# A two-layer graph attention kernel: edges counted block by block, two weight sums made by DMA, the range check moved back

## The chip, the core and the metric

The kernel runs on one core of a Trainium2 chip. Its engines are TensorE (PE; its weight loads are listed as PEld), VectorE (DVE), ScalarE (ACT), GpSimd (POOL) and SyncE (SP), each with an instruction queue of its own that is worked off in order. DMA transfers are issued from the queues of SP, ACT and POOL. The metric is the device time of one execution in microseconds. Three runs of the kernel before the change took 659.91, 660.31 and 660.65 us, so the median is 660.31 us.

## What is computed

The reference is a two-layer graph attention network (8 heads, then 1 head) on 512 nodes with 768 features, followed by a residual and a layer norm. There are 16,896 edges, sorted by destination; every node has a loop to itself.

```python
def gat_layer(x, W, a_s, a_d, b, edge_index, concat):
    h = (x @ W).reshape(n, H, C)
    src, dst = (edge_index[0], edge_index[1])
    alpha_s = jnp.einsum('nhc,hc->nh', h, a_s)
    alpha_d = jnp.einsum('nhc,hc->nh', h, a_d)
    e = jax.nn.leaky_relu(alpha_s[src] + alpha_d[dst], NEG_SLOPE)
    m = jax.ops.segment_max(e, dst, num_segments=n)
    e = jnp.exp(e - m[dst])
    denom = jax.ops.segment_sum(e, dst, num_segments=n)
    alpha = e / (denom[dst] + EPS)
    msg = h[src] * alpha[:, :, None]
    return jax.ops.segment_sum(msg, dst, num_segments=n) + b

h = jax.nn.elu(gat_layer(x, W1, a_src1, a_dst1, b1, edge_index, concat=True))   # 8 heads of 768
out = gat_layer(h, W2, a_src2, a_dst2, b2, edge_index, concat=True)             # 1 head of 768
x = _layernorm(x + out)
```

## The kernel before

**Edges become a matrix.** Instead of gathering by edge, the kernel counts how many edges lead from each source to each destination. The result `cnt` is 512 x 512; attention is then dense arithmetic on it. The edges are cut into 132 chunks of 128. DVE writes, for each chunk, a one-hot tile of the sources, `os` (128 edges x 512 nodes, L418), and for a quarter of the chunks at once a one-hot tile of the destinations, `odw` (L409). TensorE multiplies the two and adds the products up in PSUM (L430), 32 destination rows at a time, on one of four groups of 32 columns of the array (`tile_position=(0, r)`), so that products on different groups can run beside each other.

**Two blocks for every chunk.** As the edges are sorted, a chunk lies near a known destination. Nodes come in 16 blocks of 32. `first[c]` is the first of two neighbouring blocks that chunk `c` is counted into. `odw` is 64 columns wide for each chunk (`W = 2 * B`), and each chunk costs two products: 264 in all. `rel` (L201) is the destination less the first node of those blocks.

**The range check.** L203 and L205 count the edges whose `rel` is outside 0 to 63 into `stray`. A product with a column of ones (L444) sums this over the partitions, L459 copies the sum to `flag`, and L482 loads it into a register of every engine. Where it is not zero, the whole pass is done again by a general path (`flag is None`); otherwise that path is skipped.

**Order of the first stage.** The order in each queue is written out by hand. `order` lists the chunks in waves of up to four, `batches` takes four waves at a time, and the loop at L454 does for each batch: destinations if needed, the sources of its chunks, some DVE work from `extra` (sums of `x`, logits of head 0, and in the last batches `tsums`), then on TensorE the `items` that are due (the projection of head 0 and the first four pieces of that of head 1, each six matmul records; transposes of `x` by `turn_x` at the positions in `turns`), then `count`. `os` has 28 buffers: DVE can't write the 29th before TensorE has read the first. When all four rows of blocks of a `cnt` tile are done, ACT copies it out (`counted`, L337, L338). In the last batch `spread` (L363) and `lift` (L369) come ahead of the last count; then DVE does `leak` (L373) and `rank` (L378) for the softmax, and TensorE goes on with the projection of head 1.

**Strassen's products.** Projections use seven half-size products instead of eight (Winograd's form; P1 to P7). On the right-hand side they need sums of quarters of the weight matrix: T1 = B11 + B12, T3, T2 = T1 + B22, T4 = T2 + B21. `load_w` makes T1 and T3 with accumulating DMAs from POOL's queue (L104, L115); `right` returns T2 and T4 as two DVE additions (L240, L241). For head 1 these are the `tsums` that stand in batches 8 and 9 of the first stage. P6 reads T2 and P4 reads T4; both come after the first four pieces.

**The rest.** For heads 0 to 7 the kernel then aggregates (L625, L571), applies the ELU, multiplies by the head's part of the second weight matrix (L248) and projects the head after next (L248). None of this is touched, apart from its start.

**Before the first product.** TensorE runs 13 products on zeros (`keep_warm(13)`), turns the indices (L181), runs one more on zeros, transposes a tile of `x` (L327), runs two on zeros, does the range check's product (L444), runs two more on zeros, and starts the projection of head 0 (L352).

Of the kernel before, what the change touches and what calls it, by code (L numbers as in the profile page):

```python
# [36 lines left out]
def gat_pass(  # L37
# [134 lines left out]
    nc.vector.memset(far, -NO_EDGE)  # L172


    idx_f = ohp.tile([EH, 2, 2, P], F32, name="idx_f")
    nc.vector.tensor_copy(idx_f, idx_i)
    idx = ohp.tile([P, 2, EC], F32, name="idx")
    psi = tr.tile([P, 512], F32, name="tr")
    for j in range(2):
        for r in range(2):  # L180
            nc.tensor.transpose(psi[:, (2 * j + r) * EH:(2 * j + r + 1) * EH], idx_f[:, j, r, :],  # L181
                                ident[:EH, :EH])
    nc.vector.tensor_copy(idx, psi[:, :2 * EC].rearrange("p (j c) -> p j c", j=2))

    general = flag is None


    B = 32
    W = 2 * B
    first = [min(max(round(((c + 0.5) * P * N / E) / B - 1), 0), N // B - 2) for c in range(EC)]  # L190
    runs = []
    for c in range(EC):
        if not runs or first[c] != first[runs[-1][0]]:
            runs.append([c, c])
        runs[-1][1] = c + 1
    if not general:
        base = ohp.tile([P, EC], F32, name="base")
        for lo, hi in runs:
            nc.gpsimd.memset(base[:, lo:hi], float(first[lo] * B))
        rel = ohp.tile([P, EC], F16, name="rel")  # L200
        nc.vector.tensor_tensor(rel, idx[:, 0, :], base, op=ALU.subtract)  # L201
        below = ohp.tile([P, EC], F16, name="below")
        nc.vector.tensor_scalar(below, rel, 0.0, None, op0=ALU.is_lt)  # L203
        stray = const.tile([P, 1], F32, name="stray")
        nc.vector.scalar_tensor_tensor(below, rel, float(W), below, op0=ALU.is_ge, op1=ALU.add,  # L205
                                       accum_out=stray)

    cnt = keep.tile([P, NT, N], F32, name="cnt")
    absent = keep.tile([P, NT, N], BF16, name="absent")
# [24 lines left out]
    def right(W_, slot):  # L234
        lo, hi, t1 = W_
        b11, t3, b21, b22 = lo[:, :, L], lo[:, :, R], hi[:, :, L], hi[:, :, R]
        t2, t4 = (wpool.tile([P, HK, HALF], F32, name=f"{slot}t{j}") for j in (2, 4))
        tt = nc.vector.tensor_tensor
        return dict(P1=b11, P2=b21, P3=b22, P4=t4, P5=t1, P6=t2, P7=t3), [
            lambda: tt(t2, t1, b22, op=ALU.add),  # L240
            lambda: tt(t4, t2, b21, op=ALU.add),  # L241
        ]
# [76 lines left out]

    load_w1(1, "w2")()  # L320


    def turn_x(t):
        for ks in (range(4), range(4, DC)):
# [55 lines left out]
        nc.scalar.activation(q, q, AF.Exp, bias=nmax, scale=-1.0)  # L380
        return q

    order = []
    for g in range(NT):
        rs = [list(range(lo, hi)) for lo, hi in runs if lo * NT // EC == g]
        while any(rs):
            order.append([r.pop(0) for r in rs if r])
    def turn_b1():
        psb = mm.tile([P, 512], F32, name="mm")
        nc.tensor.transpose(psb[:, :H * DC], b1_rows, ident[:H * DC, :H * DC])  # L390
# [1 line left out]
        nc.scalar.activation(nb1T, psb[:, :H * DC], AF.Copy, scale=-1.0)  # L392

    XA, xsums = left(xT, xS)
    B1, tsums = right(W1[1], "w2")
    items = whole_projection(0)
    again = None
    if not general:
        hits = {}
        for c in range(EC):  # L400
            for k in range(2):
                hits[first[c] + k] = hits.get(first[c] + k, 0) + 1
        todo = dict(hits)
        cps, done = {}, 0
        od = ohp.tile([P, EC, W], BF16, name="odw", bufs=1)

        def destinations(lo, hi):
            hi = min(hi, EC)
            nc.vector.tensor_tensor(od[:, lo:hi, :],  # L409
                                    rel[:, lo:hi].unsqueeze(2).to_broadcast([P, hi - lo, W]),  # L410
                                    nodes[:, :W].unsqueeze(1).to_broadcast([P, hi - lo, W]),
                                    op=ALU.is_equal)

        def sources(wave):
            hot = {}
            for c in wave:
                hot[c] = ohp.tile([P, N], BF16, name="os", bufs=28)
                nc.vector.tensor_scalar(hot[c], nodes, idx[:, 1, c:c + 1], None, op0=ALU.is_equal)  # L418
            return hot

        def count(wave, hot):
            nonlocal done
            for k in range(2):
                for c in wave:
                    b = first[c] + k
                    t, r = b * B // P, b * B % P
                    if t not in cps:
                        pool, name = (bc, "bc") if t == 2 else (tr, "tr")
                        cps[t] = pool.tile([P, 512], F32, name=name)
                    nc.tensor.matmul(cps[t][r:r + B, :N], od[:, c, k * B:(k + 1) * B], hot[c],  # L430
                                     start=todo[b] == hits[b], stop=todo[b] == 1,
                                     tile_position=(0, r), skip_group_check=True)
                    todo[b] -= 1
            while done < NT and all(todo[b] == 0 for b in range(done * P // B, (done + 1) * P // B)):
                counted(done, cps[done])
                done += 1


        turns = {1: 3, 5: 0, 9: 1}
        keep_warm(1)  # L440
        turn_x(2)
        keep_warm(2)
        pst = tr.tile([P, 512], F32, name="tr")
        nc.tensor.matmul(pst[:1, :1], stray, ones, start=True, stop=True)  # L444
        keep_warm(2)
        wholes = len(items)

        extra = {2: xsums[:1], 4: [lambda: logits(0, HS[0], 2)],
                 5: [xsums[1], lambda: logits(0, HS[0], 3)], 6: [*xsums[2:], lambda: logits(0, HS[0], 0)],
                 7: [lambda: logits(0, HS[0], 1)], 8: tsums[:1], 9: tsums[1:]}  # L450
        BW = 4
        batches = [order[i:i + BW] for i in range(0, len(order), BW)]
        pos, ready, quarter = 0, 0, EC // NT
        for n, batch in enumerate(batches):  # L454
            while ready <= max(c for wave in batch for c in wave):
                destinations(ready, ready + quarter)
                ready += quarter
            if n == 0:
                nc.vector.tensor_copy(flag, pst[:1, :1])  # L459
            hot = [sources(wave) for wave in batch]  # L460
            for f in extra.pop(n, []):
                f()
            want = min(2 + ((n + 1) * (wholes + 4) * BW + len(order) - 1) // len(order), wholes + 4)
            while pos < want:
                if pos == wholes:
                    pairs = projection(1, XA, B1)
                    items += [lambda p=p: (p[0](), p[1]()) for p in pairs[:4]]
                if pos in turns:
                    turn_x(turns[pos])
                items[pos]()  # L470
                pos += 1
            if n == 2:
                turn_b1()
            if n + 1 == len(batches):
                spread(0)
                q = [lift(0, t) for t in range(NT)]
                for t in range(NT - 1):
                    leak(q[t])
                for t in range(NT - 1):
                    rank(q[t], t)  # L480
            if n == 1:
                again = nc.values_load(flag[:1, :1], min_val=0, max_val=E)  # L482
            for wave, h_ in zip(batch, hot):
                count(wave, h_)
        assert not extra and pos == len(items) and done == NT
    else:
        for t in range(NT):
            ps = mm.tile([P, 512], F32, name="mm")
            for c in range(EC):
                o1 = ohp.tile([P, P], BF16, name="od", bufs=4)  # L490
                o2 = ohp.tile([P, N], BF16, name="os", bufs=28)
                nc.vector.tensor_scalar(o1, nodes[:, t * P:(t + 1) * P], idx[:, 0, c:c + 1], None,
                                        op0=ALU.is_equal)
                nc.vector.tensor_scalar(o2, nodes, idx[:, 1, c:c + 1], None, op0=ALU.is_equal)
                nc.tensor.matmul(ps[:, :N], o1, o2, start=c == 0, stop=c == EC - 1)
            counted(t, ps)
            turn_x(t)
        turn_b1()
        for f in items + xsums + tsums:
            f()  # L500
        for t in range(NT):
            logits(0, HS[0], t)
        pairs = projection(1, XA, B1)
        for m, e in pairs[:4]:
            m()
            e()
        spread(0)
        q = [lift(0, t) for t in range(NT)]
        for t in range(NT - 1):
            leak(q[t])  # L510
        for t in range(NT - 1):
            rank(q[t], t)
# [426 lines left out]
```

## Time and profile before

| what | us | where from |
|---|---|---|
| median of 3 runs | 660.31 | times |
| the profiled execution's own time | 660.2 | its record |
| span, first to last instruction | 658.4 | page |
| outside the span | 1.8 | 660.2 - 658.4 |
| first product of head 0's projection starts | 8.70 | chain in order of time |
| last product of the last count but one ends | 68.1 | chain in order of time |
| product of head 1's P6 (first after the counts) starts | 69.23 | timeline |

In the profile, a time in front of a line is microseconds from the start of the span. A group's own time includes its latency, so groups of back-to-back instructions are best measured from the start of one group to the start of the next. "[3.04 <-PE tr L430]" after a line means that its engine was idle for 3.04 us just before it and that a TensorE instruction of line 430 released it. One f32 product is listed as two records.

### The profile page before, as it was taken

What the parts mean: (1) busy time and instruction counts of PE and PEld (TensorE: products, weight loads), DVE (VectorE), ACT (ScalarE), POOL (GpSimd) and SP (SyncE); (2) the same over time, 40 slices, a digit from 0 to 9 for tenths busy, and PEclk for the clock granted to TensorE, in tenths of its full rate; (3) what the DMA queues carried; (4) which work ended last, traced back from release to release, by engine and by line L of the source; (5) the groups of instructions that cost most, each with busy time, mean ns of one, the idle gap of its engine ahead of it and who ended that gap; (6) DMA issues with size and microseconds to landing.
All of it is one profiled execution on the core that took longest, in us unless ns stands there. A gap on an engine that the chain in (4) does not pass through costs nothing.

```text
span 658.4 us, 7115 instructions
## 1 busy us (share of the span) xinstructions
PE 649.1 (99%) x2419; PEld 402.0 (61%) x2419; DVE 511.2 (78%) x1102; ACT 248.7 (38%) x417; POOL 42.4 (6%) x52
## 2 busy tenths in 40 slices
PE   9999999999999999999999999999999999999995
PEld 5555577556865577556855576556755545644553
DVE  6989989977779587767779687867776589866775
ACT  2222646350635135440726135430726043333440
POOL 1200011010100110010000110011000000000000
PEclk9999999999999999999999999999999999999998
DMA  8801299177803982087604790196506865000132
GB/s 311 237 1 49 33 276 278 41 223 156 224 1 68 247 235 66 16 243 187 169 0 110 205 265 35 32 255 201 129 0 166 211 201 133 24 0 1 32 57 77
DMA packets 71355, 85.58 MB, mean 130 GB/s; under 512 B 36566, under 2 KB 55950, under 8 KB 71310
## 3 DMA queue, kind: packets, MB, share of 16 engines
q1 hardware_dynamic: 59022, 66.76, 32.6%
q0 software_dynamic: 12000, 17.70, 15.9%
q10 hardware_dynamic: 288, 0.59, 0.3%
q8 instruction: 21, 0.34, 0.2%
q14 instruction: 24, 0.20, 0.1%
HBM read 75.07 MB, written 1.57 MB: 116 GB/s over the span
## 4 chain that ended last, share of the span: by engine, by line
PE 95%; DVE 3%; ACT 0%; DMA 0%; issue 0%; DVEq 0%; ACTq 0%
PE mm L248 59%; PE mm L625 17%; PE mm L571 6%; PE mm L352 5%; PE mm L891 3%; PE tr L430 2%; PE bc L154 1%; PE bc L430 1%; PE bc L363 1%; DMA zr<-nr 0%; DVE q L373 0%; DVE q L378 0%; DVE q L528 0%; PE mm L327 0%; PE tr L819 0%
## 5 line engine op out<-in xcount | busy, mean ns | idle before, releaser
L248 PE MATMUL mm<-w,gT 128*128 128x384 f32 x288 | 97.4, 487 | 0.0
L248 PE MATMUL mm<-w,xT 128*128 128x384 f32 x252 | 83.9, 487 | 0.0
L248 PEld LDWEIGHTS mm<-w,gT 128*128 128x128 f32 x288 | 53.9, 190 | 35.7 <-issue 2.0
L248 PEld LDWEIGHTS mm<-w,xT 128*128 128x128 f32 x252 | 47.7, 190 | 33.7 <-PE bc L430 0.4
L248 PE MATMUL mm<-w1t,gS 128*128 128x384 f32 x180 | 60.7, 486 | 0.0
L380 ACT ACTIVATE q<-q,nmax 128x512 f32<-128x512 f32 x36 | 25.8, 722 | 89.8 <-DVE nmax L378 89.8
L248 PE MATMUL mm<-w2t,xS 128*128 128x384 f32 x168 | 56.6, 487 | 0.0
L625 PE MATMUL mm<-PT,hs 128*128 128x256 f32 x216 | 52.6, 379 | 0.0
L629 ACT COPY u<-mm 128x256 f32<-128x256 f32 x18 | 6.7, 372 | 119.0 <-PE mm L625 119.0
L306 DVE TENSOR_TENSOR h<-h,mm 128x384 f32<-128x384 f32 x72 | 39.6, 551 | 14.4 <-PE mm L248 13.8
L248 PEld LDWEIGHTS mm<-w1t,gS 128*128 128x128 f32 x180 | 34.1, 190 | 23.6
L248 PEld LDWEIGHTS mm<-w2t,xS 128*128 128x128 f32 x168 | 31.8, 190 | 22.2 <-issue 0.2
L625 PEld LDWEIGHTS mm<-PT,hs 128*128 128x128 f32 x216 | 41.0, 190 | 7.2 <-issue 0.4
L548 ACT COPY nr<-q 128x1024 uint16<-128x1024 uint16 x32 | 33.4, 1044 | 22.5 <-DVE q L534 15.5
L571 PE MATMUL mm<-PT,hs 128*128 128x512 f32 x96 | 41.6, 593 | 0.0
L418 DVE TENSOR_SCALAR os<-nodes,idx 128x512 bf16<-128x512 f16 x132 | 36.0, 345 | 3.0 <-PE tr L430 3.0
L553 ACT COPY PT<-zr 128x1024 uint16<-128x1024 uint16 x32 | 37.1, 1158 | 2.0 <-DMA zr<-nr 2.0
L625 PE MATMUL mm<-pS,gS 128*128 128x256 f32 x144 | 37.1, 380 | 0.2 <-DVE pS L598 0.2
L352 PE MATMUL mm<-w,xT 128*128 128x384 f32 x96 | 33.2, 493 | 0.0
L248 PE MATMUL mm<-w,gS 128*128 128x384 f32 x96 | 32.6, 486 | 0.0
L248 PE MATMUL mm<-w1t,gT 128*128 128x384 f32 x96 | 32.5, 487 | 0.0
L571 PEld LDWEIGHTS mm<-PT,hs 128*128 128x128 f32 x96 | 18.2, 190 | 22.9 <-issue 21.5
(158 smaller groups left out, 1031.5 us busy)
## 6 DMA issues: line engine op xcount, KB each, us to landing
w<-in_L_gnn_W_dram SPq DMA_DIRECT2D x90, 384.0 KB, 6.2
w<-in_L_gnn_W_dram POOLq DMA_DIRECT2D x15, 576.0 KB, 8.7
w2t<-in_L_gnn_W_dram SPq DMA_DIRECT2D x8, 576.0 KB, 4.6
w2t<-in_L_gnn_W_dram POOLq DMA_DIRECT2D x8, 576.0 KB, 8.7
w1t<-in_L_gnn_W_dram SPq DMA_DIRECT2D x7, 576.0 KB, 4.4
w1t<-in_L_gnn_W_dram POOLq DMA_DIRECT2D x7, 576.0 KB, 9.4
a_s<-in_L_gnn_a_src_dram SPq DMA_DIRECT2D x8, 384.0 KB, 3.6
a_d<-in_L_gnn_a_dst_dram SPq DMA_DIRECT2D x8, 384.0 KB, 3.6
```

The lines of the kernel that those rows point to most:

```text
L248: nc.tensor.matmul(ps[:, :HALF], A_[p][:, k, i * P:(i + 1) * P], B_[p][:, k, :], start=start and k == 0, stop=k == HK - 1, skip_group_chec ...
L306: nc.vector.tensor_tensor(a, a, ps, op=ALU.subtract if p == "P7" else ALU.add)
L352: nc.tensor.matmul(ps, xT[:, r * HK + k, t * P:(t + 1) * P], W1[h][r][:, k, cols], start=r == 0 and k == 0, stop=r == 1 and k == HK - 1)
L380: nc.scalar.activation(q, q, AF.Exp, bias=nmax, scale=-1.0)
L418: nc.vector.tensor_scalar(hot[c], nodes, idx[:, 1, c:c + 1], None, op0=ALU.is_equal)
L430: nc.tensor.matmul(cps[t][r:r + B, :N], od[:, c, k * B:(k + 1) * B], hot[c], start=todo[b] == hits[b], stop=todo[b] == 1, tile_position=(0 ...
L548: nc.scalar.copy(apart.rearrange("p (h n) -> p h n", h=2), q.bitcast(U16).rearrange("p (n h) -> p h n", h=2))
L553: nc.scalar.copy(PT.rearrange("p s n -> p (s n)").bitcast(U16).rearrange("p (s n h) -> p s n h", s=NT, h=2)[:, :, t * P:(t + 1) * P, :], p ...
L571: nc.tensor.matmul(ps[:, :N], HS[h][:, s, c * P:(c + 1) * P], PT[:, s, :], start=(s == 0), stop=(s == NT - 1))
L625: nc.tensor.matmul(bank[p][:, :HN], A_[p][:, k, c * P:(c + 1) * P], B_[p][:, k, :], start=over is None and k == 0, stop=k == 1, skip_group ...
L629: nc.scalar.copy(u, part("P1"))
L891: nc.tensor.matmul(ps[:, :cols.stop - cols.start], PT[:, s, t * P:(t + 1) * P], h2[:, s, cols], start=(s == 2), stop=(s == 1))
```

## The change

There are three parts.

1. **Blocks.** `blocks[c]` holds the one block in which the middle of chunk `c` lies, and a second one only where the middle is within 10 nodes (`SLACK`) of that block's edge. 54 chunks have one block, 78 have two: 210 columns of `rel` and 210 products. `odw` has 32 columns for each. As the number of blocks differs by chunk, the destinations are spread to 210 columns by a product with a 0/1 matrix `pick`, which DVE fills with 32 small copies of the identity; `base` takes 48 small memsets on POOL instead of 15. `count` now takes a whole batch, keeps one queue for each of the four column groups and takes one product from each in turn. `order` groups chunks by the block in which their middle lies (36 waves, 9 batches instead of 42 waves, 11 batches).
2. **Sums by DMA.** T2 and T4 of head 1 (`sums1`) are made by two plain loads in SP's queue, behind head 1's weights, and five accumulating DMAs in POOL's queue. The two DVE additions are gone from this stage. For heads 2 to 7 nothing changes.
3. **Range check.** The check counts the edges inside (`found`) in the first batch's extra work instead of those outside ahead of everything. Its product stands on TensorE in batch 1, between that batch's items and its count; DVE makes `flag` from it at the start of batch 2, ahead of that batch's sources, and the register load stands in batch 3. Two products on zeros are gone. The transpose of the second tile of `x` comes behind both halves of the first group (`turns` has 2 instead of 1).

```diff
+        B, SLACK = 32, 10
+        blocks = []
+        for c in range(EC):
+            m = (c + 0.5) * P * N / E
+            b = int(m // B)
+            lo, hi = b - (m - b * B < SLACK), b + ((b + 1) * B - m < SLACK)
+            blocks.append(range(max(lo, 0), min(hi, N // B - 1) + 1))
...
+            nc.vector.tensor_copy(pick[:, at[lo]:at[hi]].rearrange("p (c k) -> p c k", k=k),
+                                  ident[:EH, lo % EH:(hi - 1) % EH + 1].unsqueeze(2).to_broadcast([EH, hi - lo, k]))
+            for j, b in enumerate(blocks[lo]):
+                nc.gpsimd.memset(base[:, at[lo]:at[hi]].rearrange("p (c k) -> p c k", k=k)[:, :, j], float(b * B))
...
+            nc.tensor.matmul(psi[:, cols], idx_f[:, 0, r, :], pick[:, cols], start=True, stop=True)
...
+        nc.vector.tensor_tensor(rel, psi[:, :NB], base, op=ALU.subtract)
+        idx = ohp.tile([P, EC], F32, name="idx")
+        nc.vector.tensor_copy(idx, psi[:, NB:NB + EC])
...
+    sums1 = {name: wpool.tile([P, HK, HALF], F32, name=f"w2t{j}") for name, j in (("P6", 2), ("P4", 4))}
+    for n, (r, cols) in enumerate(((0, L), (0, R), (1, R), (1, L))):
+        part = w1[r * HK * P:(r + 1) * HK * P, D:2 * D][:, cols].rearrange("(k p) d -> p k d", p=P)
+        for name in ("P6", "P4") if n < 3 else ("P4",):
+            if n:
+                nc.gpsimd.dma_start(sums1[name], part, accum_op=ALU.add)
+            else:
+                nc.sync.dma_start(sums1[name], part)
...
-    B1, tsums = right(W1[1], "w2")
+    lo_, hi_, t1_ = W1[1]
+    B1 = dict(P1=lo_[:, :, L], P2=hi_[:, :, L], P3=hi_[:, :, R], P5=t1_, P7=lo_[:, :, R], **sums1)
...
+            nc.vector.tensor_tensor(od[:, lo:hi, :],
+                                    rel[:, lo:hi].unsqueeze(2).to_broadcast([P, hi - lo, B]),
+                                    nodes[:, :B].unsqueeze(1).to_broadcast([P, hi - lo, B]),
                                     op=ALU.is_equal)
+        def inside():
+            below = ohp.tile([P, NB], F16, name="below")
+            nc.vector.tensor_scalar(below, rel, float(B), None, op0=ALU.is_lt)
+            nc.vector.scalar_tensor_tensor(below, rel, 0.0, below, op0=ALU.is_ge, op1=ALU.mult, accum_out=found)
...
+        def count(batch, hot):
+            queues = [[(c, b) for wave in batch for c in wave for b in blocks[c] if b * B % P == r]
+                      for r in range(0, P, B)]
+            while any(queues):
+                for c, b in [q_.pop(0) for q_ in queues if q_]:
...
-        turns = {1: 3, 5: 0, 9: 1}
+        turns = {2: 3, 5: 0, 9: 1}
         keep_warm(1)
         turn_x(2)
         keep_warm(2)
         pst = tr.tile([P, 512], F32, name="tr")
-        nc.tensor.matmul(pst[:1, :1], stray, ones, start=True, stop=True)
-        keep_warm(2)
...
-            if n == 0:
-                nc.vector.tensor_copy(flag, pst[:1, :1])
+            if n == 2:
+                nc.vector.tensor_scalar(flag, pst[:1, :1], -1.0, float(E), op0=ALU.mult, op1=ALU.add)
...
             if n == 1:
+                nc.tensor.matmul(pst[:1, :1], found, ones, start=True, stop=True)
+            if n == 3:
                 again = nc.values_load(flag[:1, :1], min_val=0, max_val=E)
```

## The prediction, made before the changed kernel was run

> **What bounds the kernel now.** First the busy table by stretches of time. Columns: stretch and its length; busy us and instructions of PE, PEld, DVE, ACT, POOL; PE's granted clock, DMA share, GB/s.
>
> ```profile
> 8.70:24.60 15.90, 15.90 (x100) 8.93 (x103) 15.90 (x46) 3.17 (x7) 4.88 (x2) 1.00 1.01 366
> 24.60:68.90 44.30, 44.30 (x313) 22.32 (x302) 41.08 (x115) 8.99 (x20) 0.00 (x0) 1.00 0.20 43
> 68.90:90.00 21.10, 20.88 (x69) 12.25 (x66) 19.07 (x47) 14.65 (x19) 0.00 (x0) 1.00 0.46 93
> ```
>
> The stage that the change edits ends near 69 us. PE is busy throughout, but a busy PE may be one whose products wait for data, and DVE is busy for 41.1 of the second stretch's 44.3 us. So I read the timeline of DVE and PE.
>
> ```profile
> 10.17 4.27 DVE L418 TENSOR_SCALAR os<-nodes,idx 128x512 bf16<-128x512 f16 x16
> 14.37 2.34 DVE L409 TENSOR_TENSOR odw<-rel,nodes 128x2112 bf16<-128x2112 f16 x1
> 16.64 5.59 DVE L418 TENSOR_SCALAR os<-nodes,idx 128x512 bf16<-128x512 f16 x21
> 19.39 3.56 POOL L104 DMA_DIRECT2D w2t<-in_L_gnn_W_dram  x1 [16.91 <-DMA w2t<-in_L_gnn_W_dram]
> 22.16 0.94 DVE L228 TENSOR_TENSOR xS<-xT 128x768 f32<-128x768 f32 x1
> 22.50 1.77 POOL L115 DMA_DIRECT2D w<-in_L_gnn_W_dram  x1
> 23.03 4.76 DVE L418 TENSOR_SCALAR os<-nodes,idx 128x512 bf16<-128x512 f16 x16
> ...
> 36.25 1.14 DVE L418 TENSOR_SCALAR os<-nodes,idx 128x512 bf16<-128x512 f16 x4 [3.04 <-PE tr L430]
> ...
> 64.70 3.42 PE L430 MATMUL tr<-os,odw 128*32 128x512 bf16 x42
> 66.98 1.35 DVE L241 TENSOR_TENSOR w2t<-w2t,w 128x1152 f32<-128x1152 f32 x1
> 68.25 0.60 DVE L418 TENSOR_SCALAR os<-nodes,idx 128x512 bf16<-128x512 f16 x2
> 69.23 4.14 PE L248 MATMUL mm<-w2t,xS 128*128 128x384 f32 x12
> 69.46 1.90 DVE L373 SCALAR_TENSOR_TENSOR q<-q 128x512 f32<-128x512 f32 x3 [0.60 <-ACT q L369]
> ```
>
> Prices, from start to start: one os is 4.20/16 = 0.2625 us; a quarter of odw 2.27 us, or 1.08 ns an element; one sum of x (xS, xT) 0.87 (22.16 to 23.03). Read the same way in the timeline, a tile's two logits take 1.87 (43.47 to 45.34) and L240 and L241 1.26 each. At 36.25 DVE has waited 3.04 us: all 28 os buffers were full. After that its list has no gap: 67 os (17.6), 8 logits instructions (7.5), 3 sums of x (2.6), one odw (2.3) and the two T sums (2.5) make 32.5 us, and 36.25 + 32.5 = 68.75, where its last os ends (68.85). So PE and DVE are level here: PE's projection resumes at 69.23 behind the last os, and whichever of the two the change leaves longer sets the end.
>
> The chain of waits in order of time shows PE's side (start, us, what):
>
> ```profile
> 8.16 0.54 PE bc L154 x2
> 8.70 1.94 PE mm L352 x6
> 17.10 1.84 PE tr L430 x32
> 36.43 0.21 PE bc L430
> 36.64 0.23 PE tr L430 x7
> ```
>
> Six records of L352 take 1.94 us. Eight count products, two for each column group, take 0.21 + 0.23: products on one group follow each other by 0.21 us, those on different groups overlap. A batch costs its fullest group times 0.21.
>
> **Part 1, the start.** Two zero products (0.54 us, 8.16 to 8.70) and the wait for the check's product go. The index turn grows from four products (0.26) to two turns and two 105-column f32 products, two passes each: about 0.13 + 0.35 by columns, so +0.22. The first group then starts at 6.24 (end of the 13) + 0.48 + 0.21 + 0.65 + 0.42, about 8.05 instead of 8.70. Its weights allow it: the DMA issues put the first half's landing at 1.6 + 6.1 = 7.7 us and the second's near 9.3, when PE needs it at 10. **Gain on PE 0.65 us.** In DVE's queue 32 small copies stand ahead of the indices' conversion. They fit between 2.18 and 4.91, where DVE waited 2.73 us for the indices, if one takes under 0.085; PE's 13 zero products, which last to 6.24, hide it up to 0.11. The nearest row, L169, has two 128x4 reductions in 0.23, 0.115 each: 0.1 us late. The 48 memsets at 0.042 (15 in 0.63) end near 3.9, and rel needs them near 6.7. If copies and memsets excluded each other fully, the copies would end 2 us later still, and PE with them. I take 0.1 us, bounds 0 and 1.5.
>
> **Part 2, the counts.** I went through both orders batch by batch, counting each batch's products by column group. The fullest groups add up to 76 rounds before (264 products) and 59 after (210): 17 x 0.21 = **3.6 us less on PE**. On DVE: odw from 8448 to 6720 elements, 1.9 us less; the T sums, 2.5 us less.
>
> **Part 3, the check becomes a wait.** DVE now stops at L496 until PE has multiplied `found`, which stands behind batch 1's items in PE's queue. PE: 8.05 + five items x 1.94 + one turn of x 0.66 = 18.4; first count, 7 rounds, 1.4: 19.8; turn 0.66 and two items 3.9: 24.35. With the hand-over, DVE goes on at **24.5**. DVE itself: rel, idx and the first odw end near 9.2; 16 os 13.4; the check's two instructions 13.9; 12 os 17.0; then all 28 buffers are full until PE's first count at 18.4; four more os near 19.8; odw 1.86: 21.6. So it waits 2.9 us. Queued behind it: 100 os (26.25), two odw (1.86 + 1.75), four sums of x (3.5), four tiles' logits (7.5): 40.85 us. PE waits for the os, ACT for nothing new. From 24.5 on I find no full buffer, as DVE now trails PE: **24.5 + 40.85 = 65.35**, against 68.85. PE finishes its seventh batch's items near 59 and waits for os, then for the last logits (spread), so PE's 3.6 us are not what counts; DVE sets the end.
>
> **Part 4, five accumulating DMAs from POOL.** They wait for the two plain loads, which queue behind weights that take DMA to about 28 us. One transfer lands 8.7 us after issue (median); POOL's issue takes 1.3 to 3.6. P6's chain of two lands near 47, P4's of three near 55; at 3.6 + 8.7 a link 51 and 66. P6 is needed at about 66.7, P4 8 us later. DMA share from 24.6 to 68.9 is 0.20, so the transfers hide; their issue may not. Between 23.03 and 27.71, 16 os took 4.68 us instead of 4.20: beside L115's issue two os lost 0.25 each (23.31 to 23.82, 23.82 to 24.31). Beside L104's issue (19.39 to 22.95) none lost anything, and POOL took 3.56 instead of its usual 1.28. The Trainium skill, SBUF — State Buffer, section "Who interferes with whom", speaks against the change here: GpSimd, which writes such descriptors, and DVE's two-port modes (tensor_scalar among them) share a port pair as an exclusive lock, and the later one blocks fully. By the rule, if POOL always came first, DVE would lose 5 x 1.28 = 6.4 us. The two rows give 0.5 and 0; their mean over five issues is **1.2 us**, which I take, bounds 0 and 6.4.
>
> A second rule against it: TensorE: Matmul & The Clock Gate, "What's actually happening", has the clock halve after an idle window of about 3.4 us. PE's new wait ahead of spread is about 1.9 us (last logits 61.95 + 0.1, PE free near 60.2, both moving with POOL's delay), and the granted clock here is 1.00. I take nothing; a drop would cost some 1.7 us.
>
> **The sum.** DVE's last os: 65.35 + 0.1 + 1.2 = 66.65. The last product follows by 0.15, so P6 starts at 66.8 instead of 69.23: 2.4 us. DVE's softmax starts at 66.7 instead of 69.46 (2.8; the 0.6 us wait for ACT's lift is gone, as lift is done by then). Behind it PE's 60 records run without a gap to 88.7, and PE and the softmax's last sums meet at 89.93, where PE had waited 0.22 for DVE; that wait goes too: **2.6 us**. The later stages are triggered by PE's own progress and shift with it. 660.2 - 2.6 = 657.6; the median lies 0.1 above the profiled run: **657.7 us**.
>
> **Rivals.**
> - *PE sets the end.* If DVE doesn't stall at the flag and POOL costs nothing, the same walk gives a last os at 64.2, 4.7 us earlier: 655.4. For: L104's issue cost DVE nothing. Against: the queue order puts the product behind two items. 10%.
> - *Nothing measurable.* POOL costs 0.6 to 0.8 an issue, or half of that and copies that start PE 1 us late: 659.0 to 661.6. For: both rules of exclusion, 47 more small instructions at the start. Against: L104. 11%.
> - *Slower.* POOL's descriptor writing blocks DVE as the rule says: 6.4 us in place of 1.2 turns 2.6 into -2.6, 662.9. It decides from about 0.76 us an issue, where the gain is gone. For: DVE has no slack from 24.5 on, and about two thirds of its time until 47 is os. Against: the one issue that cost anything cost 0.5. 13%.
> - *The check fails and the general pass runs:* some 650 us more. Worked out from the inputs, no destination lies over 4.9 nodes from its chunk's expected middle, and the slack is 10. Under 1%.
>
> **How the numbers follow.** The forecast has the remaining 66%: 656.2 (POOL and copies cost nothing, 660.3 - 4) to 659.0. About 0.2% (1.3 us) is what a measurement of this kernel can tell from no change. Faster is the forecast and the first rival, 0.76; same 0.11; slower 0.13. The range reaches from 656.0, leaving out part of the first rival, to 660.8, which takes in most of the second.
>
> **What would show it.** os in DVE idle 2 to 3.5 us ahead of L496, released by PE L519; no buffer wait after it; last os (L454) ending near 66.7; PE waiting ahead of L392; 210 records of L468; first L381 near 8.05; POOL L347 issues between 27 and 48 us with os of up to 0.6 us beside them, and nothing else longer. Wrong would be: L347 issues each stretching several os, copies of L211 over 0.12 us, P6 or P4 waiting for DMA, or a stage from 69 to 90 that does not shift as a whole.

## The result

| | before | after |
|---|---|---|
| median | 660.49 us (12 runs) | 658.66 us (12 runs) |
| ratio of the times | 1 | 0.9974, 95% interval 0.9965 to 0.9983 |
| span of the profiled execution | 658.4 | 656.4 |
| P6's first product starts | 69.23 | 67.37 |
| TensorE goes on behind the softmax's last sums | 89.93 | 87.91 |
| from there to the end of the span | 568.5 | 568.5 |

The change gains 0.26%, 1.8 us by the medians and 2.0 us by the two profiled executions; 2.6 were forecast. The last row shows that what follows the first stage takes as long as it did, only earlier.

The same three stretches of the busy table, now of the changed kernel:

```profile
8.70:24.60 15.90, 15.44 (x75) 8.98 (x74) 11.52 (x37) 3.11 (x7) 2.69 (x2) 1.00 1.05 383
24.60:68.90 44.30, 43.52 (x285) 21.93 (x284) 43.08 (x127) 11.21 (x23) 12.41 (x5) 1.00 0.68 130
68.90:90.00 21.10, 21.01 (x69) 12.62 (x68) 19.04 (x47) 12.52 (x15) 1.28 (x1) 1.00 0.51 135
```

DVE, the third pair of columns, fell from 15.90 to 11.52 us in the first stretch: it now waits there. In the second it has almost no gap (43.08 of 44.30). POOL, the fifth, rose from 0 to 12.41 us for the five new transfers that it issues, and DMA's share from 0.20 to 0.68.

The timeline of the changed kernel shows the places that the forecast named:

```profile
1.85 1.72 POOL L214 MEMSET base<- 128x6 f32 x48
2.09 1.50 DVE L211 COPY pick<-ident 66x6 f32<-66x6 f32 x1
2.17 3.21 DVE L211 COPY pick<-ident 66x10 f32<-66x10 f32 x31
7.91 4.14 PE L381 MATMUL mm<-w,xT 128*128 128x384 f32 x12
12.08 0.48 ACT L384 COPY hs<-mm 128x384 f32<-128x384 f32 x1 [3.95 <-PE mm L381]
12.52 0.86 ACT L357 COPY xT<-mm 128x512 f32<-128x512 f32 x2
13.16 6.07 PE L381 MATMUL mm<-w,xT 128*128 128x384 f32 x18 [0.46 <-ACT xT L357]
19.59 1.45 DVE L454 TENSOR_SCALAR os<-nodes,idx 128x512 bf16<-128x512 f16 x4 [2.65 <-PE tr L468]
25.68 0.14 DVE L496 TENSOR_SCALAR flag<-tr 1x1 int32<-1x1 f32 x1 [2.77 <-PE tr L519]
25.75 3.48 DVE L454 TENSOR_SCALAR os<-nodes,idx 128x512 bf16<-128x512 f16 x13
...
41.39 4.56 DVE L454 TENSOR_SCALAR os<-nodes,idx 128x512 bf16<-128x512 f16 x16
44.44 1.87 POOL L347 DMA_DIRECT2D w2t<-in_L_gnn_W_dram  x1 [2.63 <-DMA w2t<-in_L_gnn_W_dram]
51.67 2.92 POOL L347 DMA_DIRECT2D w2t<-in_L_gnn_W_dram  x1 [5.36 <-DVE os L454]
...
63.49 3.50 DVE L454 TENSOR_SCALAR os<-nodes,idx 128x512 bf16<-128x512 f16 x13
64.03 0.65 PE L392 MATMUL bc<-ident,al_s 128*128 128x128 f32 x4 [0.63 <-ACT absent L367]
67.37 4.14 PE L268 MATMUL mm<-w2t,xS 128*128 128x384 f32 x12
```

DVE waits 2.65 us for a free os buffer and 2.77 us for the range check's product; behind the flag no DVE line up to 67 names a wait. The last os ends at 66.99 (63.49 + 3.50) and P6 starts 0.38 us later. Not forecast: TensorE waits for ACT before 13.16. Named by the forecast but not expected: the first copy of L211 takes 1.50 us beside POOL's memsets.

### The profile page after: what moved, and what is told of

Its sections match the earlier page's. It is cut to its first block, busy times and chain, and to the rows that moved or that the text cites. A ratio compares the mean times of both kernels' runs of the same rounds, so it can differ in the third digit from the quotient of the medians.

```text
span 656.4 us, 7049 instructions
## 1 busy us (share of the span) xinstructions
PE 646.2 (98%) x2365; PEld 400.6 (61%) x2365; DVE 510.2 (78%) x1132; ACT 248.5 (38%) x417; POOL 53.7 (8%) x90
## 4 chain that ended last, share of the span: by engine, by line
PE 94%; DVE 4%; ACT 1%; DMA 0%; issue 0%; ACTq 0%; DVEq 0%
PE mm L268 59%; PE mm L663 17%; PE mm L609 6%; PE mm L381 5%; PE mm L929 3%; DVE os L454 1%; PE tr L468 1%; PE bc L154 1%; DVE scr L283 1%; DMA zr<-nr 0%; PE bc L392 0%; PE bc L468 0%; PE mm L356 0%; PE tr L857 0%; DVE q L566 0%; PE tr L578 0%
## 5 line engine op out<-in xcount | busy, mean ns | idle before, releaser
L663 PEld LDWEIGHTS mm<-PT,hs 128*128 128x128 f32 x216 | 41.0, 190 | 7.2 <-issue 0.4
L104 POOL DMA_DIRECT2D w1t<-in_L_gnn_W_dram x7 | 8.9, 1277 | 307.8 <-PE mm L268 226.3
```

What stands on the lines that cost most here:

```text
L104: nc.gpsimd.dma_start(t1, upper[:, :, R], accum_op=ALU.add)
L663: nc.tensor.matmul(bank[p][:, :HN], A_[p][:, k, c * P:(c + 1) * P], B_[p][:, k, :], start=over is None and k == 0, stop=k == 1, skip_group ...
```

## The experiments

The theory after this result: **DVE's list behind the flag sets the end of the stage; TensorE's saved products are slack.** The rivals: TensorE sets it, or one part alone brings the gain.

A single profiled execution can start up to 1 us late (see the last section), so of traces I compare P6's start less the start of the first product of head 0's projection, here called the stage: 60.69 us before (69.23 - 8.54), 59.46 after (67.37 - 7.91). 8.54 is the timeline's start of that product, which overlaps the product ahead of it; the chain puts it at 8.70, so the stage is good to some 0.1 or 0.2 us. Ratios are to the kernel before, measured beside each kernel, with 95% intervals; medians of different rows come from different chips, so compare the ratios.

| kernel | median us | ratio | interval | stage us |
|---|---|---|---|---|
| changed | 658.66 | 0.9974 | 0.9965 to 0.9983 | 59.46 |
| part 1 alone | 660.62 | 1.0008 | 0.9999 to 1.0017 | 61.20 |
| part 2 alone | 659.97 | 0.9996 | 0.9987 to 1.0005 | 60.63 |
| parts 1 and 2 | 657.76 | 0.9965 | 0.9951 to 0.9979 | 58.50 |
| parts 1 and 3 | 661.29 | 1.0013 | 1.0004 to 1.0022 | 62.42 |
| changed, transposes back | 658.36 | 0.9970 | 0.9957 to 0.9982 | 59.00 |
| changed, check's product earlier | 658.54 | 0.9973 | 0.9963 to 0.9983 | 59.34 |
| changed, no accumulating DMAs | 658.26 | 0.9967 | 0.9954 to 0.9979 | 59.34 |
| changed, 53 products added | 660.78 | 1.0008 | 0.9999 to 1.0017 | 61.67 |
| three repairs | 656.44 | 0.9943 | 0.9930 to 0.9957 | 57.76 |
| three repairs, no accumulating DMAs | 656.62 | 0.9946 | 0.9932 to 0.9960 | 57.44 |
| parts 1 and 2, 40 buffers | 656.61 | 0.9947 | 0.9934 to 0.9961 | 57.24 |
| three repairs, other bank | 655.78 | 0.9930 | 0.9917 to 0.9944 | 56.68 |

### One part at a time

**Parts 1 and 3, with the sums back on DVE.** `sums1` is gone, and two additions stand in the extra work:

```diff
-                 5: [xsums[1], lambda: logits(0, HS[0], 3)], 6: [*xsums[2:], lambda: logits(0, HS[0], 0)],
-                 7: [lambda: logits(0, HS[0], 1)]}
+                 5: [xsums[1], lambda: logits(0, HS[0], 3)], 6: [*xsums[2:], lambda: logits(0, HS[0], 0), tsums[0]],
+                 7: [lambda: logits(0, HS[0], 1), tsums[1]]}
```

> Part 2 undone in the changed kernel: T2 and T4 are added by DVE again, in the third-last and second-last batch as before, and the seven transfers are gone. Theory (DVE sets the end): 2.5 us more on DVE less 0.3 us from the transfers, 2.2 us slower than the changed kernel, 660.9, slower than the kernel before. Rival (TensorE sets the end and the sums were covered): no slower than 0.3 us, 659.0.

It is slower than the kernel before (1.0013). The stage grew by 2.96 us for 2.5 us of additions: DVE has no slack there. The other 0.5 us is TensorE's clock. In this kernel TensorE waits 1.66 us for os tiles ahead of its last products, and behind that wait the granted clock, the third number from the right in the second line, was 0.50 for 3.4 us:

```profile
66.76 4.06 PE L460 MATMUL tr<-os,odw 128*32 128x512 bf16 x20 [1.66 <-DVE os L446]
67.30:70.70 3.40, 3.40 (x19) 1.09 (x17) 3.40 (x12) 0.26 (x1) 0.00 (x0) 0.50 0.26 80
```

P6 starts 0.89 us behind the last os here, 0.38 in the changed kernel, whose clock stays at 1.00. Without part 2, the rest of the change gains nothing, and with the halved clock it loses.

**Part 1 alone.** On top of that edit the range check returns to where it was:

```diff
-        turns = {2: 3, 5: 0, 9: 1}
+        turns = {1: 3, 5: 0, 9: 1}
...
         pst = tr.tile([P, 512], F32, name="tr")
+        inside()
+        nc.tensor.matmul(pst[:1, :1], found, ones, start=True, stop=True)
+        keep_warm(2)
...
-            if n == 2:
+            if n == 0:
                 nc.vector.tensor_scalar(flag, pst[:1, :1], -1.0, float(E), op0=ALU.mult, op1=ALU.add)
...
             if n == 1:
-                nc.tensor.matmul(pst[:1, :1], found, ones, start=True, stop=True)
-            if n == 3:
                 again = nc.values_load(flag[:1, :1], min_val=0, max_val=E)
```

> Part 1 alone: one or two blocks for each chunk, with the range check and the start as before and T2 and T4 added by DVE as before. Theory (DVE and TensorE were level before): DVE's list is 1.9 us shorter and TensorE's 3.6, of which DVE's counts: 2 to 2.7 us faster than the kernel before. Rival (the gain is in the transfers): within 0.5 us of the kernel before.

No gain, where 2 us or more were expected: the waits grew. DVE's waits of this kernel between 8 and 70 us (us in total, number, longest):

```profile
DVE os L446 <- PE tr L460: 4.8, 4, 2.3
```

That is 4.8 us in four waits for a free os buffer, where the kernel before had 3.0 in one. The 1.9 us that odw saves DVE went into waiting for TensorE to read os tiles, while TensorE, with 3.6 us less to do, waited at the end for DVE (its last os ends at 69.08). In this kernel, too, TensorE waits 1.66 us for os there, and its granted clock was 0.50 from 65.80 to 69.20; P6 starts 0.54 us behind the last os.

**Part 2 alone,** the kernel before with `sums1` in place of `tsums`:

> Part 2 alone: the kernel before with T2 and T4 of head 1 added by DMA. Theory (DVE and TensorE were level before): DVE's list is 2.5 us shorter, but TensorE's is not, so that only the last products' wait for os goes: 0.6 us faster than the kernel before, less what the issues cost. Rival (DVE alone was the bound): 2.5 us faster.

No gain that can be measured, as the theory has it, at the low end. DVE's last os ends 1.16 us earlier than before in a run that started 0.7 us late, but DVE then waits 2.47 us for ACT's lift, which waits for TensorE: there TensorE sets the end.

**Parts 1 and 2,** the edit of the range check from above without the one of the sums:

> Part 3 undone in the changed kernel: the range check is computed ahead of the first destinations, its product stands ahead of the projection with the two products on zeros behind it, DVE's flag is in batch 0, the register load in batch 1, and the transposes of the second tile of x are back between the halves of the first group. Blocks and transfers stay as changed. Theory (part 3 traded a late start for a wait of DVE at the flag, a bad trade): DVE loses the flag wait, the start is 0.7 us later, and the walk gives a last os 1 us earlier than in the changed kernel; the transfers' issue may take up to 1 us of it, as it did where the flag was moved: 0 to 1 us faster than the changed kernel. Rival (part 3 is what brings the gain): 0.7 us slower or more.

0.9965 against the changed kernel's 0.9974. The stage is 1 us shorter, but it begins later, and in time the two can't be told apart. So **neither part 1 nor part 2 gains alone, together they gain 2.3 us, and part 3 adds nothing that these runs can tell.** Before the change two engines were level: part 2 shortens DVE's list only, and what part 1 takes from DVE came back as waits for buffers. Part 3 alone, and parts 2 and 3 without part 1, were not run.

### Is TensorE's saving the gain?

**53 products added** to the changed kernel, one for each chunk with one block except the first chunk of all (`first_`), so that 263 are issued, against 264 before (the expectation counts that chunk too):

```diff
+                    first_ = todo[b] == hits[b]
+                    if len(blocks[c]) == 1 and not first_:
+                        nc.tensor.matmul(cps[t][r:r + B, :N], zeros[:, :B], hot[c], start=False, stop=False,
+                                         tile_position=(0, r), skip_group_check=True)
                     nc.tensor.matmul(cps[t][r:r + B, :N], od[:, at[c] + b - blocks[c][0], :], hot[c],
                                      start=todo[b] == hits[b], stop=todo[b] == 1,
                                      tile_position=(0, r), skip_group_check=True)
                     todo[b] -= 1
```

> The changed kernel with 54 more counting products on TensorE, one for each chunk with one block: a block of zeros times the same source tile, on the same column group, so that 264 products are issued as before; the counts stay the same, DVE's list too. Theory (DVE sets the end, TensorE has slack behind the flag): only the products ahead of the flag (15 of them, some 0.8 us on the fullest group) and in the last batch cost: 0.8 to 1.5 us slower than the changed kernel. Rival (the saved products are the gain): 3.6 us slower, slower than the kernel before.

It cost 2.2 us (0.9974 to 1.0008; the stage likewise), between the theory's 0.8 to 1.5 and the rival's 3.6. The part ahead of the flag is as expected: from the first product to the check's product 18.4 us instead of 17.5. Behind it, though, os buffers came free later (0.84 us of waiting at 48.65), and the last products (0.14 us) and os tiles beside POOL's issues took some more. TensorE's slack is real, but thinner than I had it: DVE can be at most 28 os tiles ahead, so a later count soon becomes a wait of DVE. The chain of the changed kernel says as much: it stays on TensorE until 51.45 and only then goes over to DVE's os tiles.

### The two losses of part 3

**Transposes back between the halves of the first group:**

```diff
-        turns = {2: 3, 5: 0, 9: 1}
+        turns = {1: 3, 5: 0, 9: 1}
```

> One edit to the changed kernel: the transposes of the second tile of x go back between the two halves of the first group (turns 1 instead of 2), so that ACT's copies of it run while TensorE has six records to do. Theory (DVE's list behind the flag sets the end, and the flag waits for TensorE): TensorE's 0.65 us wait for ACT at 12.5 us goes, the flag comes 0.6 us earlier, and with it everything behind: 0.5 to 0.7 us faster than the changed kernel, about 658.0. Rival (the end is set by DVE alone or by something later): within 0.2 us of the changed kernel, 658.7.

The check's product came 0.71 us sooner after the first product, as expected, and the stage was 0.46 us shorter. The time (0.9970) agrees with a gain of that size but doesn't prove it.

**The check's product ahead of batch 1's items:**

```diff
+            if n == 1:
+                nc.tensor.matmul(pst[:1, :1], found, ones, start=True, stop=True)
             want = min(2 + ((n + 1) * (wholes + 4) * BW + len(order) - 1) // len(order), wholes + 4)
...
-            if n == 1:
-                nc.tensor.matmul(pst[:1, :1], found, ones, start=True, stop=True)
```

> One edit to the changed kernel: the range check's product stands ahead of batch 1's items in TensorE's queue instead of behind them, so DVE's flag instruction has its operand before DVE gets there. Theory (DVE's wait of 2.8 us at the flag is on the path): the wait goes; DVE runs into the 28 os buffers instead and keeps only part of it, 1.2 us by the walk through the batches: about 657.5. Rival 1 (the wait is hidden, TensorE sets the end): no change, 658.7. Rival 2 (all of the wait is on the path): 2.8 us faster, 655.9.

The time did not move, which the first rival said; the reason is another. The timeline of DVE and POOL in this kernel:

```profile
32.74 0.35 DVE L454 TENSOR_SCALAR os<-nodes,idx 128x512 bf16<-128x512 f16 x1 [0.73 <-PE tr L468]
35.26 4.49 DVE L454 TENSOR_SCALAR os<-nodes,idx 128x512 bf16<-128x512 f16 x13
35.27 1.28 POOL L347 DMA_DIRECT2D w2t<-in_L_gnn_W_dram  x1 [2.55 <-DMA w2t<-in_L_gnn_W_dram]
38.10 1.28 POOL L347 DMA_DIRECT2D w2t<-in_L_gnn_W_dram  x1 [1.55 <-DMA w2t<-in_L_gnn_W_dram]
41.54 4.47 DVE L454 TENSOR_SCALAR os<-nodes,idx 128x512 bf16<-128x512 f16 x15
42.00 1.28 POOL L347 DMA_DIRECT2D w2t<-in_L_gnn_W_dram  x1 [2.62 <-DMA w2t<-in_L_gnn_W_dram]
46.43 0.35 DVE L454 TENSOR_SCALAR os<-nodes,idx 128x512 bf16<-128x512 f16 x1 [0.42 <-PE tr L468]
```

The flag came 3.05 us sooner after the first product (14.72 instead of 17.77). Of that, 1.44 us went into three waits, two behind full os buffers (0.73 and 0.42) and one ahead of odw (0.29), and 1.45 us into os tiles beside POOL's issues: 13 tiles took 4.49 us instead of 3.49, 15 took 4.47 instead of 4.02. Counted from the first product, the last os ended only 0.1 us earlier. One wait had covered two other losses.

**No accumulating DMAs:**

> The changed kernel without the five accumulating transfers; it leaves out the additions of T2 and T4, so that P6 and P4 of head 1 use B11 alone. Theory (descriptor writing costs DVE only what the profile shows, some 0.3 us around 44 us): 0.2 to 0.4 us faster, about 658.4. Rival (the forecast's 1.2 us, 0.25 an issue): 1.2 us faster, 657.5. Second rival (the shared port blocks as the rule says): several us faster.

0.9967 against 0.9974, 0.5 us with an uncertainty of about 1: the time does not decide. The trace does, for this order of work: from the flag to the last os DVE takes 41.21 us without the transfers and 41.31 with them. In the changed kernel the issues cost DVE 0.1 us.

### Taking the waits away

**Three repairs:** both edits from above, and 40 os buffers.

```diff
-                hot[c] = ohp.tile([P, N], BF16, name="os", bufs=28)
+                hot[c] = ohp.tile([P, N], BF16, name="os", bufs=40)
```

> The changed kernel with three repairs: the second tile's transposes between the halves of the first group, the range check's product ahead of batch 1's items, and 40 os buffers instead of 28. Theory (DVE is held by the flag, and with the flag moved by full os buffers; with both gone it works without a gap and meets TensorE): the walk has no wait of DVE and ends the counts 5 us earlier; less up to 1.5 us for the transfers' issue, which cost that much where the flag was moved: 3.5 to 5 us faster than the changed kernel, 653.7 to 655.2. Rival (TensorE sets the end as soon as DVE waits less): 1 us faster or less, 657.7.

3.8 us faster than before, 2 us faster than the changed kernel: less than expected. DVE did what the theory said: it has no buffer wait, and its last os ends at 62.14, 4.85 us earlier. But then TensorE is the bound, as the lines of this kernel show:

```profile
61.72 0.40 PE L468 MATMUL tr<-os,odw 128*32 128x512 bf16 x3
63.83 0.65 PE L392 MATMUL bc<-ident,al_s 128*128 128x128 f32 x4 [0.63 <-ACT absent L367]
64.41 1.48 PE L468 MATMUL tr<-os,odw 128*32 128x512 bf16 x20
65.23 1.89 DVE L402 SCALAR_TENSOR_TENSOR q<-q 128x512 f32<-128x512 f32 x3 [3.10 <-ACT q L398]
65.82 4.14 PE L268 MATMUL mm<-w2t,xS 128*128 128x384 f32 x12
```

DVE waits 3.10 us for ACT, which waits for TensorE's spread.

**The same without the accumulating DMAs:**

> The kernel with the three repairs without the five accumulating transfers; it leaves out the additions of T2 and T4, so that P6 and P4 of head 1 use B11 alone. Theory (an issue that meets os tiles costs DVE up to 0.5 us, but DVE is no longer alone in setting the end): 0 to 1.5 us faster than with the transfers. Rival (issues never cost anything that counts): the same within 0.3 us.

The same time: with DVE ahead, the issues cost nothing that counts.

**Parts 1 and 2 with 40 buffers:**

> Parts 1 and 2 with the range check ahead as before the change, and 40 os buffers instead of 28. Theory: DVE's four buffer waits (3.9 us together with 28 buffers) go, and TensorE comes level with DVE: 3 us faster than with 28 buffers by the walk, and 0.6 us slower than the kernel with the three repairs, as it starts 0.65 us later: 654.3 to 656. Rival (buffers don't matter, DVE only waits earlier or later): as with 28 buffers, 657.9.

0.9947 against 0.9965 with 28 buffers, and the same as the three repairs; 3 us were expected from the buffers. With 28 buffers DVE waits four times for a free one:

```profile
DVE os L454 <- PE tr L468: 3.9, 4, 2.3
```

With 40 these waits are gone; DVE's only waits left are for ACT's lift (3.40 us) and one for P7's product behind it. So buffers were what held parts 1 and 2 back, by 1.2 us, until TensorE sets the end. Of the two places for the range check tried with 40 buffers, neither is better. 40 buffers were not tried in the kernel before the change, nor in the changed kernel with the check where part 3 put it, so what buffers alone are worth there is not shown.

**Another PSUM bank.** TensorE's 0.63 us wait ahead of spread comes from sharing the bank `bc` with the third tile's counts, which ACT must read out first.

```diff
-                        pool, name = (bc, "bc") if t == 2 else (tr, "tr")
+                        pool, name = (bc, "bc") if t == 1 else (tr, "tr")
```

> The kernel with the three repairs, and the counts of the second tile instead of the third in the PSUM bank that the logits' spread uses next, so that spread doesn't wait for ACT to read the counts out. Theory (with the repairs TensorE sets the end, and its 0.63 us wait for ACT ahead of spread is on the path): 0.6 us faster than with the three repairs, 655.8, and 4.3 us faster than the kernel before. Rival (DVE still sets the end): the same within 0.2 us, 656.4.

655.78 us, 0.7% less than the kernel before. Against the three repairs the ratios (0.9930 and 0.9943) agree with the 0.6 us expected but don't prove it; the stage is 1.08 us shorter. The wait in front of L392 is gone in this kernel's timeline:

```profile
61.56 1.48 PE L468 MATMUL tr<-os,odw 128*32 128x512 bf16 x23
62.97 0.65 PE L392 MATMUL bc<-ident,al_s 128*128 128x128 f32 x4
```

This is the fastest version measured.

## Why the prediction was right

The direction, the mechanism and the size class held: the check's product became a wait of DVE (2.9 us forecast, 2.77 measured), DVE's list behind it ran without another listed wait, and its end set the stage. The 0.6 us by which the gain fell short is the sum of three terms that were mis-sized and partly cancelled: the flag 1.2 us late (0.1 of it had been put down for the copies), the list behind it, with POOL's share, 0.7 us shorter than forecast, and 0.2 us more from the last os to P6. That the sum came so close is in part luck.

| step | forecast | measured |
|---|---|---|
| first product of the projection | 8.05 | 7.91 |
| first count | 18.4 | 19.16 |
| DVE goes on at the flag | 24.5 | 25.68 |
| from the flag to the last os | 40.85 + 1.2 for POOL | 41.31 |
| last os | 66.65 | 66.99 |
| from there to P6 | 0.15 | 0.38 |
| gain where TensorE and the softmax meet | 2.6 | 2.02 |

- **The flag was 1.2 us late.** The failed term is PE's path to it in part 3, "five items x 1.94 + one turn of x 0.66". The forecast checked weights and `x` for the moved transposes, but not ACT: behind the whole first group, ACT first copies that group's result (0.48 us) and only then the transposes' (0.86 us). TensorE has nothing else to do and waits, 0.7 us with the weight load. Putting the transposes back took 0.71 us off. The rest is smaller: the first count took 1.6 instead of 1.4, turns 0.8 instead of 0.66.
- **POOL's issues cost 0.1 us, not 1.2.** The forecast took the mean of two rows, 0.5 and 0. Both outcomes occurred again: the first issue in the changed kernel took 5.04 us beside os tiles that lost nothing, while with the flag moved two issues took 1.28 and lengthened 13 os tiles by 1.0 us. So the Trainium skill's rule of an exclusive lock (SBUF — State Buffer, "Who interferes with whom") has the mechanism right in both directions, but its full price, 6.4 us for five issues, appeared nowhere; 0.5 an issue was the most. An issue that was held back ended 0.8 us behind the run of os tiles beside it (35.03 against 34.23 here, 22.95 against 22.16 before the change). What decides which side loses is not shown.
- **The start.** The first product came 0.14 us sooner than forecast, but only because TensorE's zero products ended at 5.84 in this execution instead of 6.24; counted from there, it came 0.26 us later than forecast, as the four index products, for which TensorE had to wait for the indices' conversion, took 0.62 us instead of 0.35. The copies were mis-sized twice. They follow each other by 0.07 us, less than the 0.1 forecast, but they and POOL's memsets did exclude each other, though the copies read nothing that the memsets write: the first copy starts at 2.09 and ends at 3.59, just behind the last memset (1.85 + 1.72 = 3.57), eight copies end there within 0.05 us, and every kernel here with these copies shows the same. So the sign of being wrong that the forecast named, copies over 0.12 us, did appear. It cost little: 32 copies at 0.07 would have ended near 4.4, and with the memsets in their way the conversion moved from 4.91 to 5.29.
- **Spread waits, but for something else.** The forecast had it wait for the last logits; the wait of 0.63 us is for ACT to read a count tile out of the same PSUM bank. It cost nothing there, since the last os came later. TensorE was also much less far ahead than forecast: it was free for spread at 63.40, not near 60.2, and the last logits ended at 63.57.
- **The clock.** The forecast took nothing for a drop, because the wait that it expected was shorter than the idle window that it named. The changed kernel shows no drop, and its wait was 0.63 us. The argument does not carry over: in parts 1 and 3, and in part 1 alone, a wait of 1.66 us, with one of 0.63 ahead of it, was followed by 3.4 us at half the clock. There it cost the stage 0.5 us and under 0.2 us, not the 1.7 that the forecast put on a drop.
- **Slower as a rival** needed 0.76 us an issue. It stayed away, and also in another order of work: 1.45 us in all with the flag moved, under half of the 3.8 that five issues at 0.76 make.
- **What the forecast didn't see** is how far the level engines bound the parts together: it costed parts 2 and 1 as gains of DVE (2.5 and 1.9 us) and TensorE (3.6), and took the end from their sum. Taken alone, each gained nothing that could be measured.

## What to carry to other kernels

Where two engines are level, list for each of them what the stage asks, then ask how far one may run ahead of the other: the number of buffers limits what a shortened list is worth (40 instead of 28 brought parts 1 and 2 another 1.2 us by the ratios). A transpose that is moved next to its reader loses the cover that its own readout needs; look at what stands in the third engine's queue, here ACT's. And before removing a wait, look for the waits it covers: the flag's 2.8 us hid two other losses of 1.4 us each.

## What the runs showed that was not expected

**The start of one and the same instruction list moves by over 1 us.** The 13 products on zeros begin at 1.20 in every execution and run 0.43 us apart; at some moment they go over to twice that rate, in the profiled executions at 4.35 us (part 1 alone) at the earliest, and in three kernels not before the 13 were over. They ended anywhere between 5.71 us (part 1 alone) and 6.93 (part 2 alone), and with them moved most of what follows. The profile's row of granted clocks reads 1.00 over this stretch all the same, but it measures nothing there: the trace's first clock record starts at the moment of the change (4.59 in the changed kernel, where the step from product to product falls from 0.43 to 0.22). A difference under 1 us between two profiled executions of this kernel has to be read from a point behind these products.

**POOL's issue of one accumulating DMA took from 1.28 to 5.04 us,** depending on what DVE did beside it, and DVE's 0.2625 us os tiles lost nothing at one time and 0.5 us an issue at another.

**TensorE's granted clock halved for 3.4 us behind a wait of only 1.66 us,** in the two kernels that have this wait and in no other.
